# Seven products of halves for queries, keys and values in a two-layer graph network

## The chip, the core and the metric

The kernel runs on one core of one Trainium2 chip. The metric is the device time of one execution in microseconds. Six executions of the kernel before gave a median of 2787.67 us (2785.55 to 2788.72). On this core TensorE multiplies matrices and writes the products to PSUM, eight banks of 128 partitions by 512 float32 words; VectorE and ScalarE take them out and do the elementwise work; GpSimd does a few small operations; SyncE issues the transfers. In the profile TensorE's matmuls are PE, its weight loads PEld, VectorE is DVE, ScalarE is ACT, GpSimd is POOL and SyncE is SP.

## What is computed

Input x is 128 graphs of 128 nodes with 256 features, adj 128 adjacency matrices of zeros and ones, all in float32. Layer 0 is an attention layer with eight heads of 32 features and one value matrix for each edge type; layer 1 is a graph attention network of two rounds. Each ends in a feed-forward network of 1024 hidden units.

```python
q = src @ Wq + bq;  k = src @ Wk + bk          # eight heads each
attn = softmax(q k^T / sqrt(dh))
for r in range(Wv.shape[0]):                   # only r = 0, 1 occur in adj
    v_r = src @ Wv[r] + bv[r]
    out = out + (attn * (adj == r)) @ v_r
x = ln(src + out @ Wo + bo);  x = ln(x + gelu(x @ W1 + b1) @ W2 + b2)
# layer 1: two rounds of graph attention, then
x = ln(x + h);  x = ln(x + relu(x @ w_ff1 + b_ff1) @ w_ff2 + b_ff2)
```

## The kernel before

The 16384 nodes are worked in 32 groups of four graphs, 512 nodes each. All work for a group is a set of Python generators: `projections` (queries, keys, values), `attention`, `norm`, `first_ffn` and `second_ffn`, `layer1`. Each `yield` ends a step. `in_order` takes steps from several generators in an order that is written out by hand. Nothing reorders them later: every engine carries out its instructions in the order in which these steps record them. So the lists in the main loop decide what stands behind what on each engine. One turn of the loop mixes the first feed-forward network of group g+1, the second one of group g, the graph attention of both and the projections and attention of group g+2.

`projections` (L565 to L583) makes the transposed queries and keys in four tiles of 128 by 512, each from two matmuls of 512 columns (tiles `pq`, L568) that ScalarE takes out of PSUM with the bias (L572). Then it makes the values of each of the four graphs, both relations beside each other, from two matmuls of 512 columns (tile `pv`, L578), which VectorE takes out with the bias (L582). The second relation's weights have the first's subtracted ahead of time, so the attention multiplies the softmax numerators `e` with the first and the masked ones `pm` with the difference.

`attention` makes the scores of two graphs at a time in four banks (`ps`, L596), their exponentials on ScalarE (L602), the masked copies on VectorE (L610), the denominators (`pden`, L623) and the weighted sums (`pav`, L632), the reciprocals on VectorE (L647, L649), and the output projection (`pwo`, L670). `turned` transposes a normalized group (`pt`, L297), ScalarE takes both halves out with the norm's scale and shift (L300), and VectorE forms four combinations of the halves (L386 to L389).

The feed-forward networks already work by seven products of halves instead of eight. `ffn` makes the seven products of the hidden layer, 256 columns wide (L408), into the banks `seeded`, `fa` and `fe`. A product that belongs to two results is copied out by ScalarE (L446, L453, L457) and the bank goes on accumulating; VectorE adds the copies (L463, L467). Seven further products (L417) make the output. The weights' combinations are made once, by GpSimd (L211).

PSUM is used whole: four banks in the pool `ps_s`, which the projections, scores, denominators, transposes and all of layer 1's products take in turn, and one each for `seeded`, `fa`, `fe` and `pav`.

Of the kernel before, what the change touches and what calls it, by code (L numbers as in the profile page):

```python
# [9 lines left out]
F32 = mybir.dt.float32  # L10
# [96 lines left out]
def fast_pass(ctx, tc, a, out):  # L107
# [24 lines left out]
    ps_s = ctx.enter_context(tc.tile_pool(name="ps_s", bufs=4, space=PSUM))  # L132
# [29 lines left out]
    k.constants()  # L162
    first = dict(g=0, direct=0, xt=load_xT(0))
    wq, wk = k.w("L0_gnn_Wq"), k.w("L0_gnn_Wk")
    bq, bk = k.col("L0_gnn_bq"), k.col("L0_gnn_bk")

    wv = k.tile([P, NCH, 2, D], "wv")
    for c in range(NCH):
        nc.sync.dma_start(
            wv[:, c], a["L0_gnn_Wv"][0:2, c * P : (c + 1) * P, :].rearrange("r p n -> p r n")  # L170
        )
    bv = k.row("L0_gnn_bv", 2 * D)
    first["ad"], first["x"] = load_rest(0)
    for c in range(NCH):
        nc.vector.tensor_sub(wv[:, c, 1], wv[:, c, 1], wv[:, c, 0])
    nc.vector.tensor_sub(bv[:, D:], bv[:, D:], bv[:, :D])
    bo = k.row("L0_gnn_bo")

    k.queue = nc.sync
# [12 lines left out]

    B11, B21, B22, T4, T1, T2, T3 = range(7)

    def forms(name):


        kh, nh = a[name].shape[0] // 2, a[name].shape[1] // 2
        w = k.tile([P, 7, kh // P, nh], "w_" + name)
        for i, j, h in ((B11, 0, 0), (B21, 1, 0), (B22, 1, 1), (T1, 0, 1)):  # L200
            nc.sync.dma_start(
                w[:, i],
                a[name][j * kh : (j + 1) * kh, h * nh : (h + 1) * nh].rearrange(
                    "(c p) n -> p c n", p=P
                ),
            )
        return w

    def combined(w):
        for o, p, q in ((T3, B22, T1), (T1, T1, B11), (T2, B22, T1), (T4, B21, T2)):  # L210
            nc.gpsimd.tensor_sub(w[:, o], w[:, p], w[:, q])  # L211
# [36 lines left out]
    def graph_weights():  # L248
# [6 lines left out]
        gw1T = flat(w2p.tile([P, G, P], F32, tag="spread", name="gw1T")).rearrange(  # L255
# [293 lines left out]
    def prepared(S):  # L549
        g, xr, ad = S["g"], S["x"], S["ad"]  # L550
        for p in range(G // 2):
            nc.vector.tensor_add(xr[:, pair(p)], xr[:, pair(p)], over(bo, 2))

        scr = w2p.tile([P, G, P], F32, tag="gs", name=f"scr_{g}")
        nc.vector.scalar_tensor_tensor(
            flat(scr), flat(ad), 1.0, flat(ad),
            op0=ALU.subtract, op1=ALU.mult, accum_out=c_adj[:, g : g + 1],
        )

    def projections(S):  # L560

        n, xt = str(S["g"]), S["xt"]
        for o, w, bias in (("qT", wq, bq), ("kT", wk, bk)):
            S[o] = w1p.tile([P, NCH, T], F32, tag=o, name=f"{o}_{n}")
            for m in range(NCH):  # L565
                pq = mm_tile(f"pq_{n}_{m}")
                for c in range(NCH):
                    nc.tensor.matmul(  # L568
                        pq, w[:, c, m * P : (m + 1) * P], xt[:, c, :],
# [3 lines left out]
                yield  # L573
        for b in range(G):
            S["v", b] = v = w1p.tile([P, 2 * D], F32, tag=f"v{b}", name=f"v_{n}_{b}")
            pv = mm_tile(f"pv_{n}_{b}")
            for c in range(NCH):
                nc.tensor.matmul(  # L578
                    pv, xt[:, c, b * P : (b + 1) * P], wv[:, c].rearrange("p r d -> p (r d)"),
                    start=(c == 0), stop=(c == NCH - 1),  # L580
                )
            nc.vector.tensor_add(v, pv, bv)  # L582
            yield  # L583

    def scores(S, p):
# [4 lines left out]
        pss = [ps_s.tile([P, 2, NCH, P], F32, tag="s", name=f"ps_{n}_{s}") for s in range(HC)]  # L590
# [10 lines left out]
        for s in range(HC):  # L601
            nc.scalar.activation(e[:, s], pss[s], AF.Exp, scale=SCALE)  # L602

# [11 lines left out]
    def sums(S, p):  # L615
# [6 lines left out]
        for s in range(HC):  # L622
            nc.tensor.matmul(  # L623
                pden[s * DH : (s + 1) * DH], k.ones, e[:, s], start=True, stop=True
            )
        for u in range(2):
            v = S["v", 2 * p + u]
            for c in range(NCH):
                for r, m in enumerate((e, pm)):
                    for s in range(HC):  # L630
# [5 lines left out]
                        )  # L636

# [17 lines left out]
    def attention(S):  # L655
# [3 lines left out]
        for p in range(G // 2):  # L659
            scores(S, p)  # L660
            yield
            masked(S, p)
            yield
            yield from sums(S, p)
        for p in range(G // 2):
# [8 lines left out]
            added(S, 0, p, po)  # L674
            yield

    def spread(columns, n, direct):
# [13 lines left out]
        t = w2p.tile([P, G, P], F32, tag="spread", name="spread_" + n)  # L691
# [5 lines left out]
    def edges(target, source, S, l):  # L697

        n = f"{S['g']}_{l}"
        S["att"] = s = w2p.tile([P, G, P], F32, tag="gs", name="gs_" + n)  # L700
# [5 lines left out]
        nc.vector.scalar_tensor_tensor(s, s, ALPHA, s, op0=ALU.mult, op1=ALU.max)  # L706
        nc.scalar.activation(s, s, AF.Exp)
# [13 lines left out]
    def layer1(S):  # L721
# [24 lines left out]
        yield  # L746
# [43 lines left out]
    with tc.manual_schedule(engines={ET.PE, ET.Activation, ET.DVE, ET.SP, ET.Pool}):  # L790


        for _ in range(4):
# [7 lines left out]
        prepared(first)  # L801
        in_order(
            lambda: combined(w1), (pr, 4), at, (pr, 2), at, (pr, 2), at, lambda: combined(w2), (at, 3), (pr1, 2),
            (at, 2), (pr1, 2), (at, 3), pr1, at, at1, n0, n0, pr1, at1, lambda: turned(first, 0), (at1, 2),
        )
        f1 = first_ffn(first)
        prepared(S1)
        in_order(
            gelu, lambda: combined(u1), (f1, 4), pr1, f1, f1, at1, at1, f1, pr1, f1, n0, at1, (f1, 2), n0, f1, at1,
            (f1, 3), gwu, at1, f1, gwu, f1, at1, gwu,  # L810
            f1, at1, f1, gwu, at1, lambda: combined(u2), f1, n0_, f1, n0_, (f1, 3), lambda: turned(S1, 0), n1_, (n0_, 2),
# [403 lines left out]
```

## Time and profile before

| | |
|---|---|
| median of six executions | 2787.67 us |
| the profiled execution's own time | 2788.05 us |
| its span on the core | 2786.3 us |
| TensorE matmuls busy | 2751.5 us, 99% |
| TensorE weight loads busy | 2238.4 us, 80% |
| VectorE busy | 2181.6 us, 78% |
| ScalarE busy | 1575.7 us, 57% |
| GpSimd busy | 164.5 us, 6% |
| one turn of the main loop (one group) | 85.02 us |

The span runs from the first to the last instruction of the profiled execution; 1.75 us of its own time lie around it. Matmuls overlap: the time from the start of one to the start of the next is what counts, and a single matmul's listed duration is longer. A float32 matmul is recorded as two passes, so the 256 matmuls of L578 count 512 in the profile. The length of one turn is read from two starts of the same step in neighbouring groups (the transposes before the first feed-forward network start at 966.93 and at 1051.95 us).

### The profile page before, as it was taken

The page shows a single profiled execution, that of the slowest core. Times are in us where ns is not written, and L with a number is a line of the kernel's source. Part 1 is how long each engine was busy: PE and PEld are TensorE (multiplying, and loading weights), DVE is VectorE, ACT ScalarE, POOL GpSimd, SP SyncE. Part 2 cuts the span into 40 slices and gives each one's busy share as a digit, 9 for nine tenths or more (in the row PEclk, how much of TensorE's full clock was granted, in tenths as well). Part 3 has the DMA queues.
Part 4 walks back from the last instruction along what each step waited for, and adds up shares of the span by engine and source line. Part 5 has one row for each costly group of instructions (what it writes and reads, how often), then busy time and mean ns, then how long its engine had stood idle before and what let it go on. Part 6 is the DMA issues. An engine that isn't in the chain of part 4 may idle for free.

```text
span 2786.3 us, 51902 instructions
## 1 busy us (share of the span) xinstructions
PE 2751.5 (99%) x20865; PEld 2238.4 (80%) x20865; DVE 2181.6 (78%) x5055; ACT 1575.7 (57%) x3401; POOL 164.5 (6%) x153
## 2 busy tenths in 40 slices
PE   8999999999999999999999999999999999999997
PEld 4788788887888887888878888878888888888786
DVE  6677877878787878778777878787787778787867
ACT  3555655556556556556565565565565655655653
POOL 3000000000000000000000000000000000000000
PEclk9999999999999999999999999999999999999999
DMA  6000011010111000110101110101100011101000
GB/s 176 1 24 28 20 35 35 24 35 13 35 35 35 24 32 16 35 35 25 34 13 35 35 35 24 35 12 35 35 27 32 13 35 35 35 24 35 13 12 17
DMA packets 69886, 85.96 MB, mean 31 GB/s; under 512 B 8092, under 2 KB 48392, under 8 KB 69640
## 3 DMA queue, kind: packets, MB, share of 16 engines
q1 hardware_dynamic: 68808, 82.20, 9.4%
q8 instruction: 165, 2.70, 0.4%
q14 instruction: 81, 0.66, 0.1%
q10 hardware_dynamic: 832, 0.40, 0.1%
HBM read 65.68 MB, written 16.90 MB: 30 GB/s over the span
## 4 chain that ended last, share of the span: by engine, by line
PE 95%; DVE 3%; ACT 1%; issue 0%; POOL 0%; ACTq 0%; POOLq 0%; DVEq 0%
PE po L417 16%; PE ph L408 16%; PE seeded L408 12%; PE seeded L417 12%; PE pv L578 8%; PE pq L568 8%; PE pwo L670 4%; PE pav L632 4%; PE pw L729 4%; PE pt L297 3%; PE ps L596 2%; PE pden L623 2%; PE py L742 2%; PE pg L754 2%; DVE pm L610 0%; ACT x L346 0%
## 5 line engine op out<-in xcount | busy, mean ns | idle before, releaser
L346 ACT ACTIVATE x<-x,sh,rs 128x256 f32<-128x256 f32 x388 | 201.6, 597 | 202.8 <-DVE sh L341 202.8
L332 POOL TENSOR_TENSOR rs<-rs,mhalf 128x4 f32<-128x4 f32 x129 | 139.4, 1081 | 2582.3 <-DVE rs L331 2568.1
L602 ACT ACTIVATE e<-ps 128x512 f32<-128x512 f32 x256 | 131.6, 597 | 207.9 <-PE ps L596 207.9
L578 PE MATMUL pv<-wv,xT 128*128 128x512 f32 x512 | 235.7, 593 | 2.4 <-ACT e L602 2.4
L408 PE MATMUL seeded<-yS,w_L_gnn_w_ff 128*128 128x256 f32 x768 | 204.2, 388 | 3.0 <-ACT seeded L480 2.2
L408 PE MATMUL seeded<-yS,w_L_gnn_W 128*128 128x256 f32 x768 | 203.4, 387 | 1.9 <-ACT seeded L446 0.9
L317 DVE BATCH_NORM_STATS2 st<-x 128x6 f32<-128x256 f32 x512 | 192.5, 418 | 7.8
L408 PE MATMUL ph<-yT,w_L_gnn_w_ff 128*128 128x256 f32 x768 | 196.3, 385 | 0.9 <-ACT yT L300 0.9
L408 PE MATMUL ph<-yT,w_L_gnn_W 128*128 128x256 f32 x768 | 193.2, 380 | 0.6 <-ACT yT L300 0.4
L417 PE MATMUL po<-w_L_gnn_W,hT 128*128 128x128 f32 x1536 | 190.2, 277 | 0.0
L417 PE MATMUL po<-w_L_gnn_w_ff,hT 128*128 128x128 f32 x1536 | 187.0, 275 | 0.0
L417 PEld LDWEIGHTS po<-w_L_gnn_w_ff,hT 128*128 128x128 f32 x1536 | 184.1, 192 | 3.3
L417 PEld LDWEIGHTS po<-w_L_gnn_W,hT 128*128 128x128 f32 x1536 | 181.6, 192 | 5.3
L408 PEld LDWEIGHTS seeded<-yS,w_L_gnn_w_ff 128*128 128x128 f32 x768 | 140.1, 190 | 48.7 <-issue 14.1
L408 PEld LDWEIGHTS seeded<-yS,w_L_gnn_W 128*128 128x128 f32 x768 | 138.0, 189 | 51.0 <-issue 15.5
L463 DVE TENSOR_TENSOR hT<-seeded,p 128x512 f32<-128x512 f32 x128 | 88.6, 692 | 112.7 <-PE seeded L408 110.0
L408 PEld LDWEIGHTS ph<-yT,w_L_gnn_W 128*128 128x128 f32 x768 | 143.6, 191 | 36.3 <-ACT yT L300 7.9
L408 PEld LDWEIGHTS ph<-yT,w_L_gnn_w_ff 128*128 128x128 f32 x768 | 141.2, 191 | 34.6 <-issue 14.3
L610 DVE TENSOR_TENSOR pm<-e,adj 128x512 f32<-128x512 f32 x256 | 166.6, 712 | 0.0
L578 PEld LDWEIGHTS pv<-wv,xT 128*128 128x128 f32 x512 | 92.4, 190 | 81.8 <-issue 69.8
L432 ACT ACTIVATE hT<-hT,c_L_gnn_b 128x256 f32<-128x256 f32 x256 | 109.4, 497 | 62.3 <-DVE hT L463 59.9
L702 ACT ACTIVATE gs<-spread,wh 128x128 f32<-128x128 f32 x120 | 38.3, 390 | 186.7 <-DMA spread<-hbm 186.7
(160 smaller groups left out, 6103.6 us busy)
## 6 DMA issues: line engine op xcount, KB each, us to landing
xT<-in_xT_dram SPq DMA_DIRECT2D x32, 512.0 KB, 5.9
x<-in_x_dram SPq DMA_DIRECT2D x32, 512.0 KB, 7.1
out_dram<-x SPq DMA_DIRECT2D x31, 512.0 KB, 2.9
spread<-hbm SPq DMA_DIRECT2D x59, 256.0 KB, 3.3
adj<-in_adjT_dram SPq DMA_DIRECT2D x32, 256.0 KB, 6.2
w_L_gnn_W<-in_L_gnn_W_dram SPq DMA_DIRECT2D x8, 256.0 KB, 7.1
w_L_gnn_w_ff<-in_L_gnn_w_ff_dram SPq DMA_DIRECT2D x8, 256.0 KB, 4.8
hbm<-line SPq DMA_DIRECT2D x59, 2.0 KB
```

The source lines that it names most:

```text
L317: nc.vector.bn_stats(st[:, b % 2, :], S["x"][:, b, :])
L332: nc.gpsimd.tensor_tensor(rs[:, bs], rs[:, bs], k.mhalf[:, bs], op=ALU.pow)
L346: nc.scalar.activation(x[:, b, :], x[:, b, :], AF.Identity, bias=sh[:, b : b + 1], scale=rs[:, b : b + 1],)
L408: nc.tensor.matmul(bank[:, s * TH : (s + 1) * TH], wa[:, form, 0, f * P : (f + 1) * P], m, start=start and s == 0, stop=True, skip_group_c ...
L417: nc.tensor.matmul(bank[:, s * P : (s + 1) * P], m[:, f, s * P : (s + 1) * P], wb_[:, form, f, :], start=start and s + f == 0, stop=True, ...
L568: nc.tensor.matmul(pq, w[:, c, m * P : (m + 1) * P], xt[:, c, :], start=(c == 0), stop=(c == NCH - 1),)
L578: nc.tensor.matmul(pv, xt[:, c, b * P : (b + 1) * P], wv[:, c].rearrange("p r d -> p (r d)"), start=(c == 0), stop=(c == NCH - 1),)
L602: nc.scalar.activation(e[:, s], pss[s], AF.Exp, scale=SCALE)
L610: nc.vector.tensor_mul(pm[:, s], S["e", p][:, s], S["ad"][:, pair(p), None, :].to_broadcast([P, 2, NCH, P]),)
L632: nc.tensor.matmul(pav[s * DH : (s + 1) * DH, u, c, :], v[:, d0 : d0 + DH], m[:, s, u, c, :], start=(r == 0), stop=(r == 1),)
L670: nc.tensor.matmul(po[:, s * D : (s + 1) * D], oT[:, c, b * P : (b + 1) * P], wo[:, c, :], start=(c == 0), stop=(c == NCH - 1),)
L729: nc.tensor.matmul(pw[:, :NU], yT[:, c, b * P : (b + 1) * P], wu[:, c, :], start=(c == 0), stop=(c == NCH - 1),)
```

## The change

From the third group on, a new generator `projected` takes the place of `projections`. Queries and keys together are one product of the group's nodes with a matrix of 256 by 512, and so are the two relations' values. Each is made of seven products of halves instead of eight. VectorE first makes four combinations of the halves of the transposed input (`xS`). For queries and keys, and then for values, seven products, each of two matmuls of 256 columns, go alternately into two banks of their own, `qa` and `qb`. Three products belong to two results: they are copied out (for queries and keys with the bias, by ScalarE; of the values two by ScalarE and one by VectorE), the bank goes on accumulating, and VectorE adds the copies to later products. Each product and each copy is a step of its own. The first two groups keep the plain products. For these, each graph's values are now made of four matmuls of 256 columns instead of two of 512, since the weights lie in halves.

The first relation's bias is no longer added to the values. Softmax weights add up to one, so its product with `Wo` is added to the output bias once (`output_bias`). GpSimd makes four combinations each of the query-key weights and of the value weights, and these now come before those of the second feed-forward network's first matrix.

PSUM: `ps_s` has two banks instead of four, and `qa` and `qb` have one each. The scores of two graphs take two of either. From the third group on, the denominators come after the weighted sums on TensorE. Two SBUF tiles of layer 1 have one buffer instead of two. The loop's lists are written anew: the input of group g+3 is loaded in the middle of a turn, the first half of `projected` (queries and keys) lies between the steps of the first network's hidden layer, the second half (values) between those of its output layer, and the table load for GELU comes after the first round's exponential.

```diff
-    ps_s = ctx.enter_context(tc.tile_pool(name="ps_s", bufs=4, space=PSUM))
+    ps_s = ctx.enter_context(tc.tile_pool(name="ps_s", bufs=2, space=PSUM))
...
+    def projected(S):
+        n, xt = str(S["g"]), S["xt"]
+        a11, a21, a12, a22 = (xt[:, c, h * TH : (h + 1) * TH] for c in range(2) for h in range(2))
...
+        nc.vector.tensor_sub(s3, a11, a21)
+        nc.vector.tensor_add(s1, a21, a22)
+        nc.vector.tensor_sub(s2, a22, s3)
+        nc.vector.tensor_sub(s4, a12, s2)
+        yield
...
+        for values in range(2):
...
+            def product(bank, form, m, start=False):
+                for s in range(2):
+                    if values:
+                        ops = m[:, s * P : (s + 1) * P], wv[:, form, 0, :]
+                    else:
+                        ops = wqk[:, form, 0, s * P : (s + 1) * P], m
+                    nc.tensor.matmul(
+                        bank[:, s * TH : (s + 1) * TH], *ops, start=start and s == 0, stop=True,
+                        skip_group_check=True,
+                    )
...
+            def biased(o, t, k2):
+                if values and k2:
+                    nc.vector.tensor_add(o, t, over(bv, 2))
+                elif values:
+                    nc.scalar.copy(o, t)
+                else:
+                    for c in range(2):
+                        nc.scalar.activation(
+                            o[:, c], t[:, c], AF.Identity, bias=(bq, bk)[k2][:, c : c + 1]
+                        )
+            product(x, B11, a11, True)
+            yield
+            biased(p1, x2, 0)
+            yield
+            product(y, B21, a12, True)
+            yield
+            nc.vector.tensor_add(result(0, 0), y2, p1)
+            yield
+            product(x, T2, s2)
+            yield
+            biased(p16, x2, 0)
+            yield
+            product(y, T3, s3, True)
+            yield
+            biased(p7, y2, 1)
+            yield
+            product(x, T1, s1)
+            yield
+            nc.vector.tensor_add(result(1, 1), x2, p7)
+            yield
+            product(y, T4, a22)
+            yield
+            nc.vector.tensor_add(result(0, 1), y2, p16)
+            yield
+            product(x, B22, s4)
+            yield
+            biased(result(1, 0), x2, 1)
+            yield
...
-        pss = [ps_s.tile([P, 2, NCH, P], F32, tag="s", name=f"ps_{n}_{s}") for s in range(HC)]
+        banks = ((ps_1, "qa"), (ps_1, "qb"), (ps_s, "s"), (ps_s, "s"))
+        pss = [
+            pool.tile([P, 2, NCH, P], F32, tag=t, name=f"ps_{n}_{s}")
+            for s, (pool, t) in enumerate(banks if p == 0 and S["g"] > 1 else banks[2:] + banks[:2])
+        ]
...
+        late = S["g"] > 1
+        if not late:
+            plain()
...
+        if late:
+            plain()
...
-                    pr, lambda: turned(S1, 0), pr, *(() if more else (f2_,)), f1, f2_, n3, f1, n0_, (f1, 4), n0_, (f1, 2), n3, l1, f1, f1, l1, n3,
-                    (f1, 3), pr, n3, lambda: store(st[g - 1]), f1, f1, exp, l1, l1, pr, f1, l1, f1,
-                    f1, l1, n2, f1, at, n2, at, f1, pr, pr, *((ahead,) if more else ()), (at, 3), f1,
-                    f1, pr, n1, *(() if more else (ahead,)),
-                )
+                    pr, lambda: turned(S1, 0), (pr, 2), *(() if more else (f2_,)), f1, l1, gelu, (pr, 2), f2_, n3, f1, l1, pr,
+                    n0_, f1, (pr, 2), (f1, 3), n0_, l1, f1, (pr, 2), l1, f1, n3, (pr, 2), f1, l1, f1, n3, (pr, 2),
+                    (f1, 3), n3, lambda: store(st[g - 1]), f1, (n1_, 2), exp, (at, 2), f1, (l1, 3),
+                )
+            in_order(
+                f1, (pr, 2), l1, f1, (pr, 2), at, f1, (pr, 2), l1, n2, (pr, 2), f1, n2, (pr, 2), f1, (pr, 2), f1, (pr, 2), *((ahead,) if more else ()), at, f1, n1,
+                *(() if more else (ahead,)),
+            )
...
             in_order(
-                (f2, 2), n1, pr, (n2, 2), f2, at, (f2, 2), lambda: turned(S1, 1), (f2, 2), at, (n1, 2),
-                (f2, 2), l1, at, ready, (f2, 4), l1, f2, at, f2, l1, (f2, 2), at, at, f2, at, n0, l1, f2,
-                n0, l1, gelu, f2, l1, *((f2,) if g + 3 < NG else ()),
-            )
-            n0_, f2_ = n0, f2
+                f2, at, (f2, 2), n1, at, f2, at, (f2, 2), lambda: turned(S1, 1), f2, at, (n2, 2), (f2, 2),
+                at, f2, l1, ready, (f2, 3), l1, f2, at, f2, l1, (f2, 2), at, at, f2, at, n0, l1, f2,
+                n0, l1, pr, f2, *((f2,) if g + 3 < NG else ()),
+            )
+            n0_, n1_, f2_ = n0, n1, f2
```

## The prediction

> **What bounds the kernel.** I read the busy shares and the chain first, then the waits, then one turn of the main loop.
>
> ```profile
> PE 2751.5 (99%) x20865; PEld 2238.4 (80%) x20865; DVE 2181.6 (78%) x5055; ACT 1575.7 (57%) x3401; POOL 164.5 (6%) x153
> PE 95%; DVE 3%; ACT 1%; issue 0%; POOL 0%; ACTq 0%; POOLq 0%; DVEq 0%
> 966.93:1051.95 85.02, 85.02 (x651) 69.53 (x650) 67.61 (x160) 49.02 (x107) 4.34 (x4) 1.00 0.08 29
> ```
>
> The third line is one turn cut out of the busy times: its length, then PE, PEld, DVE, ACT, POOL. PE is busy for all of its 85.02 us at full clock. The list of waits has no wait of PE's matmuls at all between 250 and 2650 us. So a turn costs what PE streams in it, and a saved pass is a saved pass, as long as nothing makes PE wait.
>
> What a pass costs is not read from the listed durations. These are the groups of the value products and of a half-wide product, and three neighbours in PE's order of time:
>
> ```profile
> L578 PE MATMUL pv<-wv,xT 128*128 128x512 f32 x512 | 235.7, 593 | 2.4 <-ACT e L602 2.4
> L408 PE MATMUL ph<-yT,w_L_gnn_w_ff 128*128 128x256 f32 x768 | 196.3, 385 | 0.9 <-ACT yT L300 0.9
> ...
> 1009.89 1.88 PE L578 MATMUL pv<-wv,xT 128*128 128x512 f32 x4
> 1011.61 1.03 PE L408 MATMUL ph<-yT,w_L_gnn_w_ff 128*128 128x256 f32 x4
> 1012.47 1.03 PE L408 MATMUL ph<-yS,w_L_gnn_w_ff 128*128 128x256 f32 x4
> ```
>
> From start to start, four passes of 512 columns take 1.72 us (0.430 each) and four of 256 take 0.86 (0.215): exactly half. The means (593 and 385 ns) hold a tail that lies over the next matmul.
>
> **What goes.** Per group, queries and keys are 4 tiles x 2 matmuls x 2 passes x 0.430 = 6.88 us, the values the same. Afterwards each is 7 products x 2 matmuls x 2 passes x 0.215 = 6.02. That is 13.76 against 12.04: 1.72 us less for each of 30 groups, **51.6 us**. In the first two groups the values' 16 passes of 512 become 32 of 256, the same stream.
>
> **What comes on the other engines.** VectorE: four combinations of 128x256 at 0.44 (L386) = 1.8; eight adds of 128x512 at 0.68 (L463, L582) = 5.4; four evictions at 0.67 go (L582): +4.5 us a turn, 72.1 of 83.3. ScalarE: eight evictions of 128x256 at 0.48 (L432 from PSUM) and two copies at 0.58 against four of 128x512 at 0.68: +2.3, 51.3 of 83.3. Neither becomes the bound, so this is free where PE has other steps between an eviction and its next use. The split steps of layer 1, the single buffers and the later GELU load move work that PE's other steps cover; I cost them at nothing, and without that cover an ACT table load would show 1.28 us.
>
> **The new waits.** I laid the new order of one turn out by hand: PE's steps at start-to-start times, the other engines behind them at their rows. What a hand-over costs shows where the old order is just in time:
>
> ```profile
> 970.38 1.03 PE L408 MATMUL ph<-yS,w_L_gnn_W 128*128 128x256 f32 x4
> 971.25 1.09 PE L408 MATMUL seeded<-yS,w_L_gnn_W 128*128 128x256 f32 x4
> 972.17 1.03 PE L408 MATMUL ph<-yT,w_L_gnn_W 128*128 128x256 f32 x4
> 973.07 1.13 PE L408 MATMUL seeded<-yS,w_L_gnn_W 128*128 128x256 f32 x4
> 974.03 1.89 PE L408 MATMUL ph<-yT,w_L_gnn_W 128*128 128x256 f32 x8
> ...
> 971.45 0.59 ACT L453 COPY p<-ph 128x512 f32<-128x512 f32 x1 [0.29 <-PE ph L408]
> 972.43 0.59 ACT L457 COPY p<-seeded 128x512 f32<-128x512 f32 x1 [0.40 <-PE seeded L408]
> ...
> 974.31 0.69 DVE L463 TENSOR_TENSOR hT<-seeded,p 128x512 f32<-128x512 f32 x1 [1.18 <-PE seeded L408]
> ```
>
> PE's stream for `ph` ends at 971.25 and ScalarE starts 0.20 later; the next copy starts 0.26 after its stream; VectorE 0.28 after. The copy that ends at 973.02 lets `seeded` start at 973.07, 0.04 late, and its stream takes 0.96 instead of 0.86. So an input that is ready exactly when due costs some 0.15, and one that is later costs its lateness more. Four places of the new order come out late.
>
> (a) *Queries and keys after the transposes of group g+1.* Count from the start of the second `pwo` (958.12 in the old turn). The normalized group is ready at 7.55 (ScalarE's L346 ends at 965.67) in both orders. Then PE has three products of 1.79, one of 0.86, the transposes from 7.95 to 8.82, a product, a product of the first network, and the third query-key product is due at 10.54. It goes into the bank that ScalarE is emptying: two yT evictions from 8.6 (1.42 the two), then two bias evictions (0.84) end at 10.85. 0.31 late plus 0.15: 0.45 at the means; with evictions back to back at 0.40 it is 0.2. Ends 0.2 and 0.5; I take 0.35.
>
> (b) *Second network's third product behind the denominators.* In the old order a value product of 1.72 and more stand between. Now `pden` is followed at once by two products of 256 (1.83 with the 0.11 of the change of tile shape) and then by the product that needs `seeded` filled, and ScalarE does this first:
>
> ```profile
> 941.22 0.60 ACT L640 ACTIVATE rd<-pden 128x512 f32<-128x512 f32 x1 [0.65 <-PE pden L623]
> 941.72 0.19 ACT L640 ACTIVATION_READ_ACCUMULATOR rd<-pden 128x1 f32 x1
> 941.81 0.65 ACT L643 ACTIVATE pden<-pden,lo 128x512 f32<-128x512 f32 x1
> 942.38 0.20 ACT L643 ACTIVATION_READ_ACCUMULATOR pden<-pden,lo 128x1 f32 x1
> ```
>
> 0.2 to see `pden`, 1.36 for these four, 0.55 for the copy: 2.1 against 1.83, so 0.27 + 0.15. Ends 0.2 and 0.5; I take 0.35.
>
> (c) *Two `s` banks.* The transposes of group g+1 before layer 1 need the two banks that the second pair of scores fills. They are due 2.93 after the scores start (scores 1.10, then 0.97 and 0.86, as in the old turn at 930.98 to 933.91). ScalarE's exponentials of the two now stand behind four normalizing operations (L346, 1.98), whose input waits for a reciprocal on VectorE (L647, 1.74), and an eviction of 0.80: the first is done about 0.15 late, the second just in time. Ends 0 and 0.45; I take 0.25.
>
> (d) *Last hidden product of the first network.* In the old order a key product of 1.72 comes before it, now nothing: VectorE's add is done 0.28 + 0.69 = 0.97 after a stream that PE covers with 0.86. Ends 0 and 0.25; I take 0.15.
>
> Against these, the old turn's own 0.06, 0.14 (lines above) and 0.14 (the same place of the second network, starts at 943.80, 944.70 and 945.66) go, since other steps now stand between. Ends 0 and 0.35; I take 0.3. Together 1.10 - 0.30 = 0.80 us a turn of new waiting, between 0.05 (0.4 - 0.35) and 1.7. So a turn gets 0.92 us shorter, x 30 = **27.6 us**.
>
> **Start and end.** Five more DMA issues ahead of the first weights at 0.5 us on SP and ScalarE's queue, while the transfers are the limit; the bias product 4 passes x 0.215; eight more GpSimd combinations of 128x256 at 0.73 to 1.17 (L69) beside VectorE, where four masked products took 5.41 us instead of 2.45 while GpSimd combined weights. Against that the second network's combinations no longer fall on the first attention (PE waited 2.2 us for `pm` at 54 to 57). Ends -3 and +5; I take +1. The input transfers (5.9 us) have some 35 us in the middle of a turn; without that cover they would stall PE by their length.
>
> **Sum.** 2788.05 - 27.6 + 1 = 2761.5 against the profiled execution's own time, which lies 0.4 above the median of the six: **2762 us**.
>
> **A rule against the change.** The Trainium skill ("Perfetto Trace Analysis", Identifying the Most-Contended Engine) says that matmul busy time tells little of the distance to the limit and that the busy share of weight loads should be read beside the flops done. The row: PEld is 80% busy, a load takes 190 ns. By that rule the change spends the scarcer thing: 24 more loads a group, 4.6 us, to 74.1 of 83.3. Were loads the limit, 4.6 - 1.72 would be lost, 30 x 2.9 = 86 us, and the kernel would take 2875. The 0.215 from start to start with a load before every pass says that they hide.
>
> **Rivals.** *PE never waits*: all four places are covered. For it: ScalarE idles 36 us a turn, and the old order has no wait at all. Then 2788 - 51.6 = 2736, or 2734 with the old losses gone. Chance 0.25.
> *The waits eat the gain*: at the upper ends, 1.7 a turn, 2787 +- 5. For it: PE's products in (a) and (b) leave tenths of a microsecond. Chance 0.11.
> *Slower, by the two `s` banks*: transposes, layer 1's products and `pden` come in pairs that used to have four banks; if PE waits for each of eight pairs as long as one eviction (0.37, L733), that is 3.0 us a turn, 30 x (3.0 - 1.72) = +38: 2826. It decides from 1.72 us a turn on. Against it: most pairs have a product of 0.86 to 1.79 between them, and ScalarE is 58% busy. Chance 0.12.
> *The half-wide passes are not half price*: by busy time over count (0.460 for 512; 204.2/768 = 0.266 for 256) a group would cost 56 x 0.266 = 14.9 against 14.7: +5 us and the waits on top, 2797 or more. The starts speak against it. Chance 0.05.
> My forecast has 0.47.
>
> **Range and chances.** The range runs from PE without waits to the waits at their upper ends with a bad start, 2734 to 2795; outside lie most of the third rival and half of the fourth. 0.2% is 5.6 us, about what a measurement of this kernel can tell from none. Faster: 0.47 + 0.25, and 0.05 of the second rival; same 0.06; slower 0.17.
>
> **What would show it.** Right: a turn near 84.1 us; `pq` and `pv` groups of 128x256 with 0.215 from start to start; short waits of PE or PEld on ScalarE before `pqqa`, `seeded` and `pt`, on VectorE before `seeded`, each below half a microsecond. Wrong: a turn of 83.3 without such waits, or waits of PE for `s` banks at `pw`, `py` and `pg`, or VectorE without idle time before the value products.

## The result and the profile after

The changed kernel takes 2780.46 us in the median (2778.32 to 2783.23), the kernel before 2787.65 (2785.55 to 2789.0). The ratio is 0.9976 (95% interval 0.997 to 0.9982): 0.24% faster, just outside the 0.2% at which the prediction put what a measurement can tell from none. 2762 had been forecast. The profiled execution's own time is 2778.65 us (2788.05 before), its span 2776.9 (2786.3). The changed kernel's executions scatter over 4.9 us, and the profiled one is among its faster ones; the shares below are made against it.

The busy shares and the chain that ended last, by engine, of the changed kernel:

```profile
PE 2724.9 (98%) x21621; PEld 2371.4 (85%) x21621; DVE 2287.3 (82%) x5296; ACT 1613.9 (58%) x3589; POOL 166.3 (6%) x161
...
PE 90%; ACT 4%; DVE 3%; issue 3%; POOL 0%; ACTq 0%; POOLq 0%; DVEq 0%
```

One turn cut out of the busy times (length, then PE, PEld, DVE, ACT, POOL, and the granted clock as the third number from the end):

```profile
968.00:1052.30 84.30, 84.10 (x676) 73.74 (x675) 71.07 (x166) 50.18 (x112) 4.14 (x4) 1.00 0.09 29
```

PE's busy time is 26.6 us less, but PE is no longer busy for all of a turn, and 3% each of the chain have gone to ScalarE and to issue. A turn is 84.30 instead of 85.02: 0.72 us less, where 0.92 had been forecast. Cut at the same step (the first product of layer 1's last sums, at 229.01 and 240.99, and 28 turns later at 2609.77 and 2601.56), the span of 2786.3 goes to 2776.9 like this:

| stretch | before | after | difference | forecast |
|---|---|---|---|---|
| 28 turns | 2380.76 | 2360.57 | -20.2 | 28 x -0.92 = -25.8 |
| ahead of them | 229.0 | 241.0 | +12.0 | |
| behind them | 176.5 | 175.3 | -1.2 | |
| both ends | 405.5 | 416.3 | +10.8 | 2 turns x -0.92 + 1 = -0.8 |

So 17.2 us are missing against the forecast: 5.6 in the turns and 11.6 at the ends, most of it at the start. (The cut does not part the work alike. Counted in matmuls, the changed kernel has one pair of scores, 1.1 us, and the bias product, 0.9, more ahead of it; behind it, 1.1 less of scores and all of the 3.4 us that the seven products save outside the 28 turns. So PE lost some 10 us ahead of the cut and some 3 behind it.)

**The turn.** From the list of PEld's waits between 250 and 2600 us (us in total, times, longest):

```profile
PEld seeded L411 <- ACT seeded L483: 23.5, 28, 0.8
...
PEld pqqa L641 <- ACT pq L660: 14.0, 28, 0.5
...
PEld seeded L411 <- ACT seeded L449: 13.7, 28, 0.5
PEld pt L300 <- ACT e L715: 11.6, 28, 0.4
PEld seeded L411 <- DVE hT L466: 11.0, 28, 0.4
```

Each occurs once a turn. The last four are the places (a), (b), (c) and (d) of the prediction, with the releasers that it named. The first is longer than any of them and costs PE nothing: only the weight load waits, and the matmul behind it starts at 983.18, 0.11 after the small product ahead of it (983.07), as in the kernel before (980.09 and 980.20). So this list shows where to look, and what a wait costs is read from PE's starts in one turn:

```profile
969.74 1.03 PE L411 MATMUL ph<-yT,w_L_gnn_W 128*128 128x256 f32 x4
970.87 1.13 PE L641 MATMUL pqqa<-xS,w_qk 128*128 128x256 f32 x4
971.84 1.03 PE L411 MATMUL ph<-yS,w_L_gnn_W 128*128 128x256 f32 x4
...
986.64 1.03 PE L411 MATMUL ph<-yT,w_L_gnn_W 128*128 128x256 f32 x4
987.66 1.13 PE L411 MATMUL seeded<-yS,w_L_gnn_W 128*128 128x256 f32 x4
988.72 1.17 PE L709 MATMUL ps<-qT,kT 32*128 32x128 f32 x32
...
1014.88 1.03 PE L411 MATMUL ph<-yS,w_L_gnn_w_ff 128*128 128x256 f32 x4
1015.99 1.13 PE L411 MATMUL seeded<-yS,w_L_gnn_w_ff 128*128 128x256 f32 x4
1016.96 1.03 PE L411 MATMUL ph<-yT,w_L_gnn_w_ff 128*128 128x256 f32 x4
...
1019.99 1.03 PE L411 MATMUL ph<-yT,w_L_gnn_w_ff 128*128 128x256 f32 x4
1021.03 1.14 PE L300 MATMUL pt<-ident,x 128*128 128x128 f32 x8
1022.01 1.03 PE L411 MATMUL ph<-yT,w_L_gnn_w_ff 128*128 128x256 f32 x4
```

Four passes of 256 columns take 0.86 from start to start when nothing is late. At (a) the product starts 0.27 late (970.87 against 970.60) and its own stream takes 0.97 instead of 0.86: 0.38 together by these rows, 0.37 by the length of a turn without it (E6). In the same way (b) is 0.25 and 0.11, 0.36; (c) 0.18 and 0.10, 0.28 (eight passes of the transposes take 0.88 elsewhere); (d) 0.16 and 0.10, 0.26 (of the 1.06 there, 0.96 also pass between 1016.96 and the scores at 1017.92, where nothing is late).

**The start.** GpSimd from 66 to 88 us, VectorE's masked products, and PE around the weighted sums of the second group's first pair (start, duration, instruction, waiting time before it), all of the changed kernel:

```profile
70.32 2.65 POOL L184 TENSOR_TENSOR w_v<-w_v 128x256 f32<-128x256 f32 x3 [16.65 <-PE pv L590]
72.93 13.44 POOL L184 TENSOR_TENSOR w_L_gnn_w_ff<-w_L_gnn_w_ff 128x512 f32<-128x512 f32 x8
...
75.12 3.43 DVE L367 TENSOR_TENSOR x<-x,r_L_gnn_g 128x512 f32<-128x512 f32 x2
78.48 6.76 DVE L725 TENSOR_TENSOR pm<-e,adj 128x512 f32<-128x512 f32 x4
...
75.74 1.07 PE L740 MATMUL pden<-e,ones 128*32 128x512 f32 x8
76.62 0.40 PE L754 MATMUL pav<-e,v 128*32 128x128 f32 x8
80.28 0.41 PE L754 MATMUL pav<-pm,v 128*32 128x128 f32 x2 [3.25 <-DVE pm L725]
81.95 0.63 PE L754 MATMUL pav<-pm,v 128*32 128x128 f32 x2 [1.26 <-DVE pm L725]
83.62 0.63 PE L754 MATMUL pav<-pm,v 128*32 128x128 f32 x2 [1.04 <-DVE pm L725]
85.30 0.42 PE L754 MATMUL pav<-pm,v 128*32 128x128 f32 x1 [1.04 <-DVE pm L725]
...
88.31 1.13 PE L411 MATMUL seeded<-yS,w_L_gnn_W 128*128 128x256 f32 x4
```

The combinations of the value weights are made in place, so they wait until PE has read the plain weights for the last time: GpSimd stands still for 16.65 us. What stands behind them in its queue starts at 72.93: the eight combinations of the second network, 13.44 us long. They now run on top of the second masked products. Those take 6.76 us instead of 2.49, and PE waits 6.6 us for them. From the denominators' start to the next hidden product are 12.57 us. The same two lines and the masked products in the kernel before:

```profile
76.48 2.49 DVE L610 TENSOR_TENSOR pm<-e,adj 128x512 f32<-128x512 f32 x4
...
77.02 1.07 PE L623 MATMUL pden<-e,ones 128*32 128x512 f32 x8
...
80.67 1.13 PE L408 MATMUL seeded<-yS,w_L_gnn_W 128*128 128x256 f32 x4
```

There it is 3.65. PE's granted clock falls too. In the stretch from 76 to 88.4 us the kernel before has 1.00, the changed one 0.72 (third number from the end):

```profile
76.00:88.40 12.40, 5.80 (x73) 3.37 (x65) 11.52 (x8) 2.04 (x6) 9.98 (x7) 0.72 0.00 0
```

**The two `s` banks, in the first and the last turn.** There PE waits for ScalarE to empty a bank of layer 1's products (`pw`, `py`) before it can make the second pair of them. The longest of these waits in the changed kernel:

```profile
128.34 2.02 PE L862 MATMUL pw<-wu,yT 128*128 128x260 f32 x8 [1.58 <-ACT wh L866]
142.92 1.14 PE L875 MATMUL py<-wh,gs 128*128 128x258 f32 x4 [1.12 <-ACT yh L878]
...
2714.72 1.14 PE L875 MATMUL py<-wh,gs 128*128 128x258 f32 x4 [1.87 <-ACT yh L878]
```

With two shorter ones at the end (0.25 and 0.30) they are 5.1 us. The kernel before, with four banks, has none of them.

### The profile page after: what moved, and what is told of

Its sections match the earlier page's. It is cut to its first block, busy times and chain, and to the rows that moved or that the text cites. A ratio compares the mean times of both kernels' runs of the same rounds, so it can differ in the third digit from the quotient of the medians.

```text
span 2776.9 us, 54158 instructions
## 1 busy us (share of the span) xinstructions
PE 2724.9 (98%) x21621; PEld 2371.4 (85%) x21621; DVE 2287.3 (82%) x5296; ACT 1613.9 (58%) x3589; POOL 166.3 (6%) x161
## 4 chain that ended last, share of the span: by engine, by line
PE 90%; ACT 4%; DVE 3%; issue 3%; POOL 0%; ACTq 0%; POOLq 0%; DVEq 0%
PE po L420 16%; PE ph L411 13%; PE seeded L411 13%; PE seeded L420 12%; PE pqqa L641 4%; PE pwo L789 4%; PE pw L862 4%; PE pvqa L641 4%; PE pav L754 4%; PE pt L300 3%; PE pvqb L641 3%; PE pqqb L641 3%; PE ps L709 2%; PE py L875 2%; PE pg L888 2%
## 5 line engine op out<-in xcount | busy, mean ns | idle before, releaser
L335 POOL TENSOR_TENSOR rs<-rs,mhalf 128x4 f32<-128x4 f32 x129 | 133.3, 1034 | 2553.2 <-DVE rs L334 2309.5
L435 ACT ACTIVATE hT<-hT,c_L_gnn_b_ff 128x256 f32<-128x256 f32 x256 | 110.1, 514 | 34.0 <-DVE hT L466 29.7
L420 PEld LDWEIGHTS seeded<-w_L_gnn_W,hT 128*128 128x128 f32 x1024 | 124.3, 192 | 3.5 <-DVE hT L517 0.3
```

The source lines that it names most:

```text
L335: nc.gpsimd.tensor_tensor(rs[:, bs], rs[:, bs], k.mhalf[:, bs], op=ALU.pow)
L420: nc.tensor.matmul(bank[:, s * P : (s + 1) * P], m[:, f, s * P : (s + 1) * P], wb_[:, form, f, :], start=start and s + f == 0, stop=True, ...
L435: nc.scalar.activation(o[:, s], o[:, s] if src is None else src[:, s * TH : (s + 1) * TH], func, bias=ba[:, f : f + 1],)
```

## The experiments

Of the lists of steps, the cuts show only the part that changes. Theory S for the start: what it lost is the price of GpSimd's combinations on top of VectorE's work. Rival T: it is the new order of the start's other steps. For the turn, the theory is that each of the four waits is a separate hand-over that order alone can cover; the rivals are that a wait taken away only turns up at the next late release. All ratios are to the kernel before, with 95% intervals; gains are differences of medians to the changed kernel's 2780.46.

**E1: the value weights' combinations last.** GpSimd makes the second network's combinations ahead of those that wait.

```diff
-  lambda: combined(wqk), lambda: combined(wv), lambda: combined(u1), f1, n0, at1,
+  lambda: combined(wqk), lambda: combined(u1), f1, n0, at1,
...
-  lambda: combined(u2), f1, n0_, pr,
+  lambda: combined(u2), lambda: combined(wv), f1, n0_, pr,
```

> GpSimd's combinations of the value weights are put behind those of the second network's two matrices (order: queries/keys, second network's first and second matrix, values); nothing else changes. Theory S (the start): in the changed kernel the value combinations wait until 70.3 us for TensorE's last plain value product, the second network's eight combinations stand behind them and run from 72.9 to 86.4 us on top of the second masked products (6.76 us for four instead of 2.49), and TensorE loses about 9 us there. Without that the gap between the second denominators' start (75.74) and the product after the weighted sums (88.31) falls from 12.6 to about 4 us, and the first masked products (53.3 us) take up to 6 us instead of 2.7, which costs 2 to 4 us: 2772 to 2777 us. Rival T (the turn): the shortfall against the forecast is all in the turn's waits, and the start is neutral: 2779 to 2782 us.

Measured: 2777.3 (ratio 0.9962, 0.9949 to 0.9976), 3.2 us gained: 0.3 above the range of Theory S, 1.7 below that of Rival T. The trace tells why. The combinations went back to where the kernel before has them:

```profile
54.37 12.20 POOL L184 TENSOR_TENSOR w_L_gnn_w_ff<-w_L_gnn_w_ff 128x512 f32<-128x512 f32 x8
...
54.76 6.45 DVE L725 TENSOR_TENSOR pm<-e,adj 128x512 f32<-128x512 f32 x4
```

The first masked products pay instead of the second ones (6.45 instead of 2.69 in the changed kernel). The collision was moved, not removed. So 3.2 us is what its new place costs more than its old one.

**E2: the second network's combinations after the second attention.**

```diff
-  lambda: combined(wqk), lambda: combined(wv), lambda: combined(u1), f1, n0, at1,
+  lambda: combined(wqk), lambda: combined(wv), f1, n0, at1,
...
-  lambda: combined(u2), f1, n0_, pr, n0_,
+  f1, n0_, lambda: combined(u1), lambda: combined(u2), pr, n0_,
```

> The second network's combinations of both matrices are put behind the root of the second group's first norm on GpSimd, so they run from about 107 us on; nothing else changes. Theory S: no masked product is slowed, the 9 us come back, and the slowed VectorE of the first turn gives 0 to 4 us of it back: 2771 to 2775 us. Rival T: 2779 to 2782 us.

Measured: 2776.41 (0.9959, 0.9945 to 0.9972), 4.1 gained; Theory S had expected at least 5.5. The first query-key product of the third group starts at 102.73 instead of 110.91, so 8.2 us were back by then. But the combinations now ran from 102.24 to 113.35, beside the next stretch of VectorE's work:

```profile
102.24 11.11 POOL L184 TENSOR_TENSOR w_L_gnn_w_ff<-w_L_gnn_w_ff 128x512 f32<-128x512 f32 x8
...
112.26 1.37 DVE L392 TENSOR_TENSOR yS<-yT,yS 128x256 f32<-128x256 f32 x1
...
106.60 1.10 PE L641 MATMUL pqqa<-xS,w_qk 128*128 128x256 f32 x4 [1.97 <-POOL w_L_gnn_w_ff L184]
```

A combination of `yS` takes 0.42 elsewhere and 1.4 here. By the first product of layer 1 the lead is down to 3.6 (120.36 against 123.99).

**E5: the same combinations by VectorE, in a stretch where it is idle.**

```diff
-    def combined(w):
+    def combined(w, engine=nc.gpsimd):
...
-  lambda: combined(wqk), lambda: combined(wv), lambda: combined(u1), f1, n0, at1,
+  lambda: combined(wqk), lambda: combined(wv), f1, n0, at1,
...
-  at1, lambda: combined(u2), f1, n0_, pr, n0_,
+  at1, f1, n0_, pr, n0_,
...
-  f1, n1_, (pr, 2), (f1, 3), lambda: turned(S, 1),
+  f1, n1_, lambda: combined(u1, nc.vector), lambda: combined(u2, nc.vector), (pr, 2), (f1, 3), lambda: turned(S, 1),
```

> The second network's eight combinations of weights leave GpSimd and are made by VectorE, at the start of the first turn, in a stretch of 5.4 us in which VectorE is idle in the trace of the changed kernel (118.04 to 123.39; eight subtractions of 128x512 at some 0.6 us from start to start take 4.9). Theory S (what the start lost is the price of GpSimd's combinations on top of VectorE's work): e2 regained 8.2 us by the first query-key product (102.73 against 110.91) and gave 4.5 back where the combinations then ran; without a second collision all 8.2 stay: 2780.4 - 8.2 = 2772, 2770.5 to 2774. Rival T (the start lost its time to the new order of its steps, and the place of the combinations matters little): 2775 to 2778, as e1 and e2.

Measured: 2772.81 (0.9946, 0.9932 to 0.9959), 7.6 gained, as Theory S expected. Against E1, with the combinations on GpSimd in their old place, it is 4.5 less: that is what the old place costs. On VectorE the eight subtractions take 5.64 us together, and the addition behind them starts without a wait:

```profile
108.27 5.64 DVE L184 TENSOR_TENSOR w_L_gnn_w_ff<-w_L_gnn_w_ff 128x512 f32<-128x512 f32 x8
113.83 0.68 DVE L466 TENSOR_TENSOR hT<-seeded,p 128x512 f32<-128x512 f32 x1
...
74.44 2.48 DVE L725 TENSOR_TENSOR pm<-e,adj 128x512 f32<-128x512 f32 x4
```

**E9: the collision in the kernel before.** Nothing but the place of the combinations is changed there; the extra subtraction of 128x1 feeds nothing.

```diff
+        def gate():
+            tiny, v = k.tile([P, 1], "tiny"), S1["v", G - 1]
+            nc.gpsimd.tensor_sub(tiny, v[:, :1], v[:, :1])
...
-  gelu, lambda: combined(u1), (f1, 4), pr1, f1, f1, at1, at1, f1, pr1, f1, n0, at1,
+  gelu, (f1, 4), pr1, f1, f1, at1, at1, f1, pr1, gate, lambda: combined(u1), lambda: combined(u2), f1, n0, at1,
...
-  at1, lambda: combined(u2), f1, n0_,
+  at1, f1, n0_,
```

> The kernel before, with one thing changed: GpSimd's eight combinations of the second network's weights wait for the second group's last value tile (a subtraction of 128x1 on GpSimd makes them wait), so that they run from some 73.5 us on, on top of the second masked products, as they do in the changed kernel. Theory S: the second masked products then cost what they cost there, some 9 us of PE's time (from the denominators' start to the next hidden product 12.57 us against 3.65), and the first ones get back what the combinations cost them in the kernel before, 2.2 us of waits (0.94 and 1.26) and some 1.7 of a lower granted clock (0.94 and 0.85 over 16 us): 2788 + 9 - 4 = 2793, 2790 to 2796. Rival T (the order of the other steps costs the time, not these combinations): 2783 to 2788.

Measured: 2793.3 (1.0021, 1.0012 to 1.003), 5.5 slower than the kernel before (2787.75 beside it): Theory S. The lines are those of the changed kernel over again:

```profile
68.35 12.96 POOL L211 TENSOR_TENSOR w_L_gnn_w_ff<-w_L_gnn_w_ff 128x512 f32<-128x512 f32 x8
...
75.11 6.76 DVE L610 TENSOR_TENSOR pm<-e,adj 128x512 f32<-128x512 f32 x4
...
71.33 1.06 PE L623 MATMUL pden<-e,ones 128*32 128x512 f32 x8
76.91 0.64 PE L632 MATMUL pav<-pm,v 128*32 128x128 f32 x2 [4.29 <-DVE pm L610]
85.04 1.58 PE L408 MATMUL seeded<-yS,w_L_gnn_W 128*128 128x256 f32 x4
```

From the denominators to the next hidden product are 13.71 us, 10.1 more than before. And the denominators start 5.7 earlier (71.33 against 77.02); 0.5 of that it already had before the combinations' old place (a value product starts at 47.26 against 47.73). So the combinations cost the kernel before some 5 us in their old place, near the 4.5 of E1 against E5.

**E3: wait (a), the third query-key product one step later.**

```diff
-  f1, l1, gelu, (pr, 2), f2_, n3, f1, l1, pr,
+  f1, l1, gelu, f2_, n3, f1, (pr, 2), l1, pr,
```

> Only the place of one step changes: the third query-key product (which waits for ScalarE, wait (a), 0.37 us a turn) comes after the first network's second product. Theory: ScalarE's chain through the GELU table load is the local limit; the copy that the fourth hidden product needs ends at 975.14 for a start at 975.29, with no slack left, so the wait of 0.37 moves there: a turn of 84.2 to 84.3 us, 2778 to 2781 us in all. Rival (the waits add up independently): 29 x 0.37 = 10.7 us less, 2769 to 2771 us, a turn of 83.9.

Measured: 2780.33 (0.9976, 0.9966 to 0.9985), nothing gained. Wait (a) is gone from the list, and another has its size:

```profile
PEld seeded L411 <- ACT p L460: 14.4, 28, 0.8
PEld seeded L411 <- ACT seeded L449: 13.8, 28, 0.5
...
```

ScalarE's chain from the transposes through an exponential, the table load (1.28 us) and three evictions had been just as late, hidden behind the first wait.

**E6: wait (a) and that chain together.** The exponential moves ahead of the transposes, into 1.05 us in which ScalarE is idle.

```diff
-  pr, lambda: turned(S1, 0), (pr, 2), *(() if more else (f2_,)), f1, l1, gelu, (pr, 2), f2_, n3, f1, l1, pr,
+  pr, l1, lambda: turned(S1, 0), (pr, 2), *(() if more else (f2_,)), f1, gelu, f2_, n3, f1, (pr, 2), l1, pr,
```

> Wait (a) taken out without handing it on: the third query-key product after the first network's second product, as in e3, and the exponentials of the attention's weights ahead of the transposes, in ScalarE's idle 1.05 us there (967.59 to 968.64), so that the table load and the copies that follow end 0.6 us earlier. Theory: the wait moved in e3 because ScalarE's chain through the table load was as late as PE; with 0.6 us less in it the turn loses 0.37 us: 29 x 0.37 = 10.7, so 2769.7, 2768 to 2773. Rival: the chain is limited by the transposes and not by what lies behind them, and nothing changes: 2779 to 2782.

Measured: 2770.2 (0.9937, 0.9923 to 0.9951), 10.3 gained. The turn is 83.93: 0.37 less, all of wait (a).

**E7: wait (b), the second pass over the denominators one step later.**

```diff
+        if late and p == 0:
+            yield
...
-  f2, at, (f2, 2), n1, at, f2, at, (f2, 2), lambda: turned(S1, 1),
+  f2, (at, 2), (f2, 2), n1, at, f2, at, (f2, 2), lambda: turned(S1, 1),
```

> Wait (b) taken out: of the denominators' two ScalarE passes the second one runs behind the copy that the second network's third product waits for, for the first pair of attention only. Theory: 0.36 us less per turn, 29 x 0.36 = 10.4, so 2770, 2768 to 2773. Rival: the next late release, the one of the transposes before layer 1 behind the exponentials (0.28 in the changed kernel), takes up what is won, so that 0.1 or less is left per turn: 2777 to 2781.

Measured: 2772.35 (0.9944, 0.993 to 0.9957), 8.1 gained. The turn is 84.01, 0.29 less; the wait for the copy L449 is 5.5 us in 28 turns instead of 13.7, so a remainder of it stays.

**E4: wait (c), one product of the second network ahead of the transposes.**

```diff
-  (f2, 2), lambda: turned(S1, 1), f2, at, (n2, 2), (f2, 2),
+  (f2, 3), lambda: turned(S1, 1), at, (n2, 2), (f2, 2),
```

> Only the place of one step changes: the transposes before layer 1, which wait for the exponentials to free the two banks (wait (c)), come one product of the second network later. Theory: 0.28 us a turn goes, 29 x 0.28 = 8 us: 2771 to 2774 us, a turn of 84.0. Rival: the transposed group then comes later to ScalarE and the wait moves to the next user of a bank: 2779 to 2782 us.

Measured: 2771.6 (0.9943, 0.993 to 0.9957), 8.9 gained, turn 84.01: 0.29 less.

**E8: wait (d), the scores' products between the last two hidden products.** The scores get a step of their own ahead of their exponentials; the first turn's list, which has one step more for it, is left out.

```diff
+        if p == 0 and S["g"] > 1:
+            yield
...
+            if p == 0 and S["g"] > 1:
+                next(parts)
+                yield
...
-  (f1, 3), n3, lambda: store(st[g - 1]), f1, (n1_, 2), exp, (at, 2), f1, (l1, 3),
+  (f1, 3), n3, lambda: store(st[g - 1]), at, f1, (n1_, 2), exp, at, f1, at, (l1, 3),
```

> Wait (d) taken out: the first scores' products, which had followed it, run between the last two hidden products of the first network, so that VectorE's addition has 1.1 us more. Theory: 0.26 us less per turn, 29 x 0.26 = 7.5, so 2773, 2771 to 2776. Rival: ScalarE's exponentials and the copy behind the first output product, now later by 0.9, make the second output product late by as much as was won: 2779 to 2783.

Measured: 2793.88 (1.0023, 1.0014 to 1.0032), 13.4 slower than the changed kernel; the turn is 84.77. Wait (d) is gone, but two others came:

```profile
PEld pvqb L641 <- DVE pv L655: 11.5, 28, 0.4
PEld seeded L420 <- DVE hT L517: 5.6, 28, 0.2
...
1001.74 0.69 DVE L843 SCALAR_TENSOR_TENSOR gs<-gs 128x512 f32<-128x512 f32 x1 [1.71 <-ACT gs L839]
...
1012.91 1.13 PE L641 MATMUL pvqb<-w_v,xT 128*128 128x256 f32 x4 [0.22 <-DVE pv L655]
```

The time lies outside both ranges. The rival had looked for the price at ScalarE's copy behind the first output product. By the trace (no run tests it) it is one step further: the later exponentials make the attention's weights of layer 1 late, VectorE stands idle for 1.71 us in front of them (1.05 before), and from there on it has hardly a gap for 15 us, so every eviction that PE needs comes later. What looked like VectorE's idle time was its reserve, by this reading.

**X1: E4, E5, E6 and E7 together.** 

> The remedies of e4, e5, e6 and e7 together. If they add up: 2780.4 - 8.8 (e4) - 7.6 (e5) - 10.2 (e6) - 8.1 (e7) = 2745.7, 2743 to 2749. Rival: with three waits gone from a turn the next late releases appear (ScalarE's chain through the table load, the second network's copies), and a quarter of the turn's gain is lost: 2752 to 2755.

Measured: 2743.03 (0.984, 0.9826 to 0.9853). The turn is 83.35, which is 84.30 - 0.37 - 0.29 - 0.29 exactly: the waits are independent and add up. The time is 2.7 below the sum of the four gains, just inside the range.

**X2: X1, and two waits of the first turn taken out.**

```diff
-  (pr, 2), f1, (n0_, 2), f1, l1, f1, (n1_, 2), l1, l1, f1, l1,
-  (f1, 2), (l1, 2), (pr, 2), f1, l1,
+  (pr, 2), f1, f1, (n0_, 2), l1, f1, (n1_, 2), l1, l1, f1, l1,
+  f1, (pr, 2), f1, (l1, 2), f1, l1,
```

> The kernel of the run before it, and in the first turn two waits of PE taken out by order alone: the scaling of 2.5 us on VectorE goes behind the first network's addition that it had delayed (the products of layer 1 waited 1.58 us there), and a query-key product stands between the first network's second and third product (0.67). Theory: 2.2 us less than the run before it. Rival: the two waits of 1.49 and 1.12 behind the attention's weights, which come next on the same chain, grow by as much: no difference.

Measured: 2740.53 (0.983, 0.9817 to 0.9844), 2.5 us below X1. Both waits are gone from PE's list (`pw` behind `wh`, 1.70 in X1, and `seeded`, 0.67), and the next one, `py` behind the attention's weights `gs`, grew from 1.50 to 2.36: the rival happens too, but takes back only a part.

**X3: X2, and another cover for wait (d).**

```diff
-  f1, n3, (pr, 2), (f1, 3), n3, lambda: store(st[g - 1]), f1,
+  f1, n3, (f1, 2), (pr, 2), f1, n3, lambda: store(st[g - 1]), f1,
```

> The kernel of the run before it, with wait (d) filled by a query-key product instead of the scores: that product goes from ahead of the first network's fourth and fifth products to behind them, so that VectorE's addition has 0.86 us more and no exponential moves. Theory: of the 0.26 us per turn some 0.1 goes into a wait of the fifth product for the copy of its bank (ends 984.89, product wanted at 984.91) and some 0.15 is left: 28 x 0.15 = 4 us less. Rival: the keys come 0.8 us later and the scores wait for them, 0.1 to 0.3 us per turn: up to 4 us more.

Measured: 2740.49 (0.9829, 0.9815 to 0.9842), no difference from X2. The turn is 83.30 against 83.35. Both hand-overs that the expectation feared are there (PEld's waits):

```profile
PEld ps L709 <- ACT kT L660: 9.7, 28, 0.7
...
PEld seeded L411 <- ACT p L460: 7.8, 28, 0.5
```

X2 and X3 are the fastest: 1.7% below the kernel before, 1.4% below the changed one. Some 5 us of the former are not the change's: taking the combinations off GpSimd (E5) also ends what they cost the kernel before in their old place. That was not run in the kernel before.

## Why the prediction was right or wrong

**The saving was right.** A half-wide pass costs half: `pqqa` at 969.31 and the product behind it at 970.17 in E6 are 0.86 apart for four passes. A turn lost 1.72 us of stream: without three of the four waits (X1) it is 83.35, where 85.02 - 1.72 - 0.34 (the old turn's own waits) + 0.33 (what is left, (d) and 0.07 of (b)) is 83.29.

**The rule against the change did not hold here.** Weight loads went from 80% to 85% busy, and in X2 to 87%, while a turn got shorter. The loads hide: four passes follow each other in 0.86, a load of some 0.19 before each.

**The four waits were right in place and releaser, nearly right in size.** Forecast 0.35, 0.35, 0.25 and 0.15, measured 0.37, 0.36, 0.28 and 0.26; recovered from the old order 0.30 forecast, 0.34 measured (in the changed kernel's turn those starts are 0.86 apart). Net 0.93 instead of 0.80. That leaves 0.07 of the turn's 0.20 unaccounted for. The term most mis-sized is (d). Its lateness had been worked out (0.97 against 0.86, 0.11) but not the 0.15 of the hand-over that the prediction itself had read off. E4 and E6 remove (c) and (a) and gain what they cost; E7 gains 0.29 of the 0.36 of (b). So for the half of the gain that the waits take, cause and size are shown, for (d) only the size.

**The step that failed is "Start and end", taken at +1 with ends of -3 and +5.** The two ends lost 11.6 us more than forecast. The prediction had the right row (four masked products 5.41 us beside GpSimd's combinations instead of 2.45) and the right observation that the second network's combinations leave the first attention. It booked that as a gain of up to 2.2 and did not ask where they go. GpSimd takes its work in order, the value combinations wait for PE's last plain value product, and the second network's combinations, held up behind them, come to lie beside the second masked products. Moving them there is a loss and no gain: 5.5 us where it is the only change (E9), 3.2 by putting them back in the changed kernel (E1). Against a gain of 2.2 that is 5.4 to 7.7 of the 11.6. The 7.6 of E5 is more than the move: it also takes away what the combinations cost in either place, some 5 us in the kernel before.

The rest, 4 to 6 us, is Rival T's: waits at the ends that the prediction put at nothing. The 5.1 us for the two `s` banks stand there in the trace, and of these only the first is tested: X2 takes 1.58 and 0.67 away in the first turn by order alone and gains 2.5 (a difference of medians). What VectorE's scaling delays there is an addition that ScalarE waits for (1.71 us, until 127.13), and the copy that frees the bank stands behind it. How the rest divides stays open.

The sum has a slip besides: 2761.5 less the 0.4 that it names is 2761.1, not 2762.

**The rivals.** "PE never waits" put the kernel at 2736 or 2734. X2, with three of the four waits and the start's collision gone, reaches 2740.5, some 5 of it from the collision that the kernel before has too; so that rival describes nearly what the edit is worth when its order is finished. "The waits eat the gain" put the kernel at 2787 +- 5 by waits of 1.7 a turn; they cost 1.27, and a third of the miss lies in the turns, two thirds at the ends. Of "slower, by the two `s` banks", which counted eight waits of 0.37 in every turn, only (c) came in the turns; the banks showed in the first and the last turn, 5.1 us in all.

## What to carry to other kernels

Where a step that has to wait is put into an in-order queue, follow everything queued behind it to the new time at which it runs, and see what runs beside it there: here 13 us of "free" GpSimd work, moved by one in-place operation that waited, cost some 8 us of TensorE's time in their new place. Ask as well what they cost in the old one, here some 5 us.

A just-in-time hand-over costs PE the lateness and here 0.1 on the stream besides; four of them a turn took over half of what the seven products saved, and reordering alone gave most of it back.

Taking a wait away uncovers the next one (E3), and an engine's idle time ahead of a busy stretch may be what keeps that stretch on time (E8); so follow the chain behind each moved step to the point where it is early by more than the shift.

## What the runs showed of the hardware that was not expected

**VectorE and GpSimd take turns.** In the collision, four masked products take 6.76 us, 1.69 each, and eight combinations 13.44, 1.68 each: one rhythm for both, though a masked product alone takes 0.62 (2.49 for four) and four such combinations took 5.30 at 15.92 in the kernel before, 1.32 each. The Trainium skill ("SBUF — State Buffer", Who interferes with whom) says that a VectorE instruction with two inputs in SBUF contends with a GpSimd instruction that reads SBUF, for a shared pair of ports that is an exclusive lock. The common rhythm agrees with it, and so does E5, where VectorE does the same subtractions at 0.7 each. That the combinations cost the kernel before some 5 us was not expected either: its waits for `pm` show only 2.2, and E9's expectation had 4.

**PE pays twice for such a wait.** After the waits its weighted sums run at half speed for 3 us. In the changed kernel eight passes take 0.43 from start to start (85.51 to 85.94, 85.94 to 86.36), in the kernel before 0.22. The granted clock in E9 is 0.50 between 78 and 84 us, behind a wait of 4.29 and through three of 1.0:

```profile
78.00:84.00 6.00, 3.35 (x44) 2.30 (x48) 5.06 (x5) 0.00 (x0) 3.18 (x2) 0.50 0.00 0
```

The Trainium skill ("TensorE: Matmul & The Clock Gate", What's actually happening) describes two states of the clock, half and full, by how busy PE was just before; the 0.50 and the doubled step agree.
